# Row biases folded into beta, freer row transposes, longer planned latencies and a new load order in a two-layer graph network

## The chip, the cores and the metric

The kernel runs on one core of one Trainium2 chip. The metric is the device time of one execution in microseconds (us), and every comparison is by the median of several executions. The lines called profile come from one execution recorded by the hardware profiler, whose own time is given beside its span.

## The reference, cut to what matters

There are 64 graphs of 256 nodes with 256 features in fp32, and an adjacency matrix of small integers for each. Two layers follow each other. The first is a graph attention network of two attention steps with a residual, a layer norm, a feed-forward part of 1024 hidden features with ReLU, and a layer norm. The second is a relational attention of 8 heads, and the same feed-forward part with GELU.

```python
# layer 0: two graph attention steps, then a feed-forward part
h = _gat(x, adj, W1, a1, Fout)
h = _gat(h, adj, W2, a2, W2.shape[1])
h = _layernorm(residual + h, g_ln1, b_ln1)
residual2 = h
ff = jnp.matmul(jax.nn.relu(jnp.matmul(h, w_ff1) + b_ff1), w_ff2) + b_ff2
return _layernorm(residual2 + ff, g_ln2, b_ln2)
...
# layer 1: attention over heads with masks by relation, then a feed-forward part
attn_out = out.transpose(0, 2, 1, 3).reshape(Bb, Nn, Dm) @ Wo + bo
x = _ln(src + attn_out, g1, beta1)
ff = jax.nn.gelu(x @ W1 + b1, approximate=False) @ W2 + b2
return _ln(x + ff, g2, beta2)
```

Three biases are added to whole rows just before a residual sum: `b_ff2`, `bo` and `b2`. They are what the change moves.

## The kernel before, in words

The work is cut into 32 pairs of graphs, and everything of a pair stays in SBUF from its loads to its output. All weights are loaded once at the start. The program is straight-line code: it has no loop at run time.

**Stages of a pair.** `whole_way` chains them. `gat_layers` makes the first layer's product (L227), transposes the exponentials `rise` of its scores (L199), weighs (L206, L207) and scales the rows (L212), makes the second layer's first product (L241), repeats the transposes and weights, and ends in the product L253, the residual sum `add_rows` (L266) and `layernorm` (L273 to L282). `feed_forward` first transposes the rows (`rows_transposed`, L289, with ACT's copy to `yT` at L290), makes 8 hidden blocks (L308, with ACT's ReLU or GELU at L311), and four products of the second matrix (L319), again with `add_rows` and `layernorm`. `attention` transposes the rows in the same way, projects queries and keys (L342), values (L335), and goes through four groups of heads: scores (L360), exp on ACT (L365), masking on VectorE (L374), sums (L381), products (L388), and the output product (L405) with a layer norm. A second `feed_forward` and the store of the rows end the pair.

**Where the biases are.** `transposed` has GpSimd (POOL) add the row bias to the residual rows (L292) after the transposes read them, so that the readers of the transposed rows see rows without it.

**The order of the work.** Each pair is a Python generator that yields after every step a tuple (us, later, needs): what the step costs TensorE, how long its result needs until the pair's next step can follow, and the name of a stage that only one pair may be in. `in_turn` keeps three pairs going and issues, step by step, the next of one that is ready by these figures, and takes one outside the feed-forward stage first. The names are "gat", "ff" and "attention"; a pair holds one until `done_with`. So the planner's figures set the order in which instructions of several pairs stand in each engine's queue; the engines then run them in that order, and wait where the figures were too short. In the steady state before, two pairs go through their stages in each 213.4 us.

**Buffers.** `x` and `adjT` have four, `xT` one, `yT` two, `ff` nine, `v` two; `ps` are the eight banks of PSUM.

**The start.** SP's queue first loads pair 0 (`xT`, `adjT`, `x`), then the weights that the setup multiplies (L119), then all layer-norm vectors, then the matrices. `load(pair + 1)` is issued after a pair's first products, so that of pair 1 comes behind the whole list. Each load on the queue also waits for the one that stands eight places ahead of it.

Of the kernel before, what the change touches and what calls it, by code (L numbers as in the profile page):

```python
# [18 lines left out]
P = 128  # L19
# [10 lines left out]
def two_layers(ctx: ExitStack, tc: tile.TileContext, t: dict, out: bass.AP, flag: bass.AP):  # L30
# [32 lines left out]
        nc.sync.dma_start(x, t["x"][rows].rearrange("b (c p) d -> p (b c) d", p=P))  # L63
        return xT, adjT, x

    loaded = {0: load(0)}


    ident = const.tile([P, P], F32, name="ident")
    make_identity(nc, ident)  # L70
# [33 lines left out]
    with tc.tile_pool(name="setup", bufs=1) as setup, \  # L104
# [11 lines left out]
        for m in range(KC):  # L116
# [2 lines left out]
                nc.tensor.matmul(pw[:, :D + 4], lhsT=w1T[:, c, m * P:(m + 1) * P], rhs=right[:, c],  # L119
                                 start=c == 0, stop=c == KC - 1)  # L120
            nc.vector.tensor_copy(w12[:, m], pw[:, :D + 4])
    ln = [tuple(on_all(n, D) for n in names) for names in (
        ("L0_gnn_g_ln1", "L0_gnn_b_ln1"), ("L0_gnn_g_ln2", "L0_gnn_b_ln2"),
        ("L1_gnn_g1", "L1_gnn_beta1"), ("L1_gnn_g2", "L1_gnn_beta2"))]
    ff0 = (weights("L0_gnn_w_ff1"), column("L0_gnn_b_ff1"), weights("L0_gnn_w_ff2"), on_all("L0_gnn_b_ff2", D))
    wq, wk, wo = weights("L1_gnn_Wq"), weights("L1_gnn_Wk"), weights("L1_gnn_Wo")
    wv = const.tile([P, KC, 2, D], F32, name="wv")
    for c in range(KC):
        nc.sync.dma_start(wv[:, c], t["L1_gnn_Wv"][:2, c * P:(c + 1) * P, :].rearrange("r p m -> p r m"))
        nc.vector.tensor_tensor(wv[:, c, 1], wv[:, c, 1], wv[:, c, 0], ALU.subtract)  # L130
    bq, bk = column("L1_gnn_bq"), column("L1_gnn_bk")
    bqs = const.tile([P, KC], F32, name="bqs")
    nc.vector.tensor_scalar(bqs, bq, SCALE, None, ALU.mult)
    bv, bo = on_all("L1_gnn_bv", 2 * D), on_all("L1_gnn_bo", D)
    nc.vector.tensor_tensor(bv[:, D:], bv[:, D:], bv[:, :D], ALU.subtract)
    ff1 = (weights("L1_gnn_W1"), column("L1_gnn_b1"), weights("L1_gnn_W2"), on_all("L1_gnn_b2", D))

    work = ctx.enter_context(tc.tile_pool(name="work", bufs=1))
    small = ctx.enter_context(tc.tile_pool(name="small", bufs=6))
# [1 line left out]

    def bank():
        return psum.tile([P, 512], F32, name="ps")

# [68 lines left out]
    def gat_layers(pair, xT, adjT, x):  # L215
        nc.vector.tensor_reduce(most[:, pair], adjT.bitcast(U32), axis=AX.X, op=ALU.max)
        empty = small.tile([P, 4], F32, name="empty")
        nc.vector.tensor_scalar(empty, most[:, pair], 0.0, EVEN, ALU.is_le, ALU.mult)
        y = work.tile([P, 4, D + 4], F32, name="xw", bufs=2)
        z = work.tile([P, 4, D + 4], F32, name="xw", bufs=2)  # L220
        a, e = [], []
        for b in range(2):
            for j in range(2):
                k = 2 * b + j
                ps = bank()
                for c in range(KC):
                    nc.tensor.matmul(ps[:, :D + 4], lhsT=xT[:, c, k * P:(k + 1) * P], rhs=w12[:, c],  # L227
                                     start=c == 0, stop=c == KC - 1)
                nc.scalar.activation(y[:, k], ps[:, :D + 4], AF.Copy)  # L229
            a.append(addends(y, D + 2, 0, pair, b))  # L230
            yield 1.75, b * 1.6, None
        if pair + 1 < NPAIR:
            loaded[pair + 1] = load(pair + 1)
        for b in range(2):
            e.append(gat_weights(y, D + 2, *a.pop(0), adjT, empty, b))
            yield 0.5, b * 3.4, None
        for b in range(2):
            for i in range(2):
                ps = bank()
                for j in range(2):  # L240
                    nc.tensor.matmul(ps[:, :D + 2], lhsT=e[b][:, j, i * P:(i + 1) * P], rhs=y[:, 2 * b + j, :D + 2],  # L241
                                     start=j == 0, stop=j == 1)
                nc.scalar.activation(z[:, 2 * b + i, :D + 2], ps[:, :D + 2], AF.Copy)
            a.append(addends(z, D, 1, pair, b))
            yield 1.75, 0.4 + b * 0.6, None
        for b in range(2):
            e.append(gat_weights(z, D, *a.pop(0), adjT, empty, b))
            yield 0.5, b * 3.4, None
        for b in range(2):
            ps = bank()  # L250
            for i in range(2):
                for j in range(2):
                    nc.tensor.matmul(ps[:, i * D:(i + 1) * D], lhsT=e[2 + b][:, j, i * P:(i + 1) * P],  # L253
                                     rhs=z[:, 2 * b + j, :D], start=j == 0, stop=j == 1)
            add_rows(x, ps, b)
            layernorm(x, ln[0], b)
            if b == 0:
                yield 1.75, 0.4, None
        done_with("gat")
        yield 1.75, 4.5, "ff"  # L260


    def add_rows(y, p, b):
# [2 lines left out]
        nc.vector.tensor_tensor(rows, p, rows, ALU.add)  # L266

    def layernorm(r, gb, b):
        g, beta = gb
        st, mv = small.tile([P, 2, 6], F32, name="st"), small.tile([P, 2, 2], F32, name="mv")  # L270
        rstd = small.tile([P, 2], F32, name="rstd")
        for j in range(2):
            nc.vector.bn_stats(st[:, j, :], r[:, 2 * b + j, :])  # L273
            nc.vector.bn_aggr(mv[:, j, :], st[:, j, :])
        nc.vector.tensor_scalar(rstd, mv[:, :, 1], EPS, None, ALU.add)  # L275
        nc.gpsimd.tensor_tensor(rstd, rstd, mhalf[:, :2], ALU.pow)  # L276
        for j in range(2):
            row = r[:, 2 * b + j, :]
            nc.vector.scalar_tensor_tensor(row, row, mv[:, j, 0:1], g, op0=ALU.subtract, op1=ALU.mult)
        for j in range(2):  # L280
            row = r[:, 2 * b + j, :]
            nc.vector.scalar_tensor_tensor(row, row, rstd[:, j:j + 1], beta, op0=ALU.mult, op1=ALU.add)  # L282

    def transposed(y, yT, bias, b):

        pt = bank()
        for c in range(KC):
            for j in range(2):
                nc.tensor.transpose(pt[:, c * N + j * P:c * N + (j + 1) * P], y[:, 2 * b + j, c * P:(c + 1) * P], ident)  # L289
        nc.scalar.activation(yT[:, :, b * N:(b + 1) * N], pt.rearrange("p (c n) -> p c n", c=KC), AF.Copy)  # L290
        for j in range(2):
            nc.gpsimd.tensor_tensor(y[:, 2 * b + j, :], y[:, 2 * b + j, :], bias, ALU.add)  # L292

    def rows_transposed(y, bias):
        yT = work.tile([P, KC, 512], F32, name="yT", bufs=2)
        for b in range(2):
            transposed(y, yT, bias, b)
            yield 0.5, 0.5 + b * 0.5, None
        return yT

    def feed_forward(y, w, func, gb):
        w1, b1, w2, b2 = w
        yT = yield from rows_transposed(y, b2)
        f = []
        for m in range(NF):
            p1 = bank()
            for c in range(KC):
                nc.tensor.matmul(p1, lhsT=w1[:, c, m * P:(m + 1) * P], rhs=yT[:, c, :],  # L308
                                 start=c == 0, stop=c == KC - 1)
            h = work.tile([P, 512], F32, name="ff", bufs=NF + 1)  # L310
            nc.scalar.activation(h, p1, func, bias=b1[:, m:m + 1])  # L311
            f.append(h)
            yield 1.72, 0.0, None
        for b in range(2):
            p2 = bank()
            for j in range(2):
                k = 2 * b + j
                for m in range(NF):
                    nc.tensor.matmul(p2[:, j * D:(j + 1) * D], lhsT=f[m][:, k * P:(k + 1) * P], rhs=w2[:, m, :],  # L319
                                     start=m == 0, stop=m == NF - 1)  # L320
                if k < 3:
                    if j == 1:
                        add_rows(y, p2, b)
                        layernorm(y, gb, b)
                    yield 3.44, 0.0, None
        add_rows(y, p2, 1)
        layernorm(y, gb, 1)
        done_with("ff")
# [16 lines left out]
    def attention(y, pair, adjT):  # L345


        yT = yield from rows_transposed(y, bo)
        qT, kT, oT = (work.tile([P, KC, 512], F32, name=n) for n in ("qT", "kT", "oT"))

        def values_tile():
# [72 lines left out]
        for n, (b, c) in enumerate(groups):  # L424
# [7 lines left out]
            if not last:  # L432
                e, ms = ahead, of_relation_1(groups[n + 1][0], ahead)
            divided(b, c, po)
            yield 3.1 if last else 4.1, 3.2 if last else 0.8, None
            if (b, c) == (0, KC - 1):
                v = values_tile()
                for jc in range(2):
                    values(v, jc, N + jc * P, yT)
                    yield 1.72, 0.0, None  # L440
            if n == 2:
                into_rows(0)
                yield 1.75, 0.0, None
        into_rows(1)
        done_with("attention")
        yield 1.75, 4.5, "ff"

    def whole_way(pair):
        yield 0.0, 0.0, "gat"
        xT, adjT, x = loaded.pop(pair)  # L450
        yield from gat_layers(pair, xT, adjT, x)
        yield from feed_forward(x, ff0, AF.Relu, ln[1])
        yield 3.44, 4.5, "attention"
        yield from attention(x, pair, adjT)
        yield from feed_forward(x, ff1, AF.Gelu, ln[3])
        nc.sync.dma_start(out[2 * pair:2 * pair + 2].rearrange("b (c p) d -> p (b c) d", p=P), x)
        yield 3.44, 0.0, None
# [410 lines left out]


_COLUMNS = ("L0_gnn_b_ff1", "L1_gnn_bq", "L1_gnn_bk", "L1_gnn_b1")  # L870


# [24 lines left out]
```

## Time and profile before

| what | us |
|---|---|
| median of 10 executions (3450.32 to 3454.75) | 3453.95 |
| the profiled execution | 3450.91 |
| its span, first to last instruction | 3449.1 |
| TensorE (PE) busy | 3344.3 |
| VectorE (DVE) busy | 1904.3 |
| ScalarE (ACT) busy | 1371.0 |
| GpSimd (POOL) busy | 481.6 |
| DMA queue of the loads and stores, mean share of the 16 engines | 6.9% |

How to read it: busy is the time in which an engine has an instruction running. Matmuls overlap in their pipeline, so their own durations add up to more than the time they take in a row; the distance from one start to the next is the better measure. PEld is the loading of TensorE's weights. A line such as L308 names the source line of the kernel; `out<-in` names the tiles. In a list of waits, an arrow leads from the waiting tile to the one that released it.

### The profile page before, as it was taken

How to read it: one execution, taken by the hardware profiler on the slowest of the kernel's cores; microseconds unless marked ns; L12 is line 12 of the kernel's file. 1: busy time of each engine (PE TensorE's matmuls, PEld its weight loads, DVE VectorE, ACT ScalarE, POOL GpSimd, SP SyncE). 2: the span in 40 equal slices, each digit the busy share in tenths (PEclk: the TensorE clock that was granted, in tenths of full speed). 3: DMA queues.
4: the chain of work that ended last, by engine and by line, in shares of the span. 5: the costliest groups of instructions: out<-in, count | busy, mean ns of one | idle time of the engine just before them, and what ended most of it. 6: DMA issues, size and time to landing. Idle time of an engine off the chain costs nothing.

```text
span 3449.1 us, 47284 instructions
## 1 busy us (share of the span) xinstructions
PE 3344.3 (97%) x18698; PEld 2150.4 (62%) x18698; DVE 1904.3 (55%) x4825; ACT 1371.0 (40%) x2586; POOL 481.6 (14%) x646
## 2 busy tenths in 40 slices
PE   7999999999999999999999999999999999999998
PEld 5566665666656566565665666656666566565655
DVE  5655645556456564555645555465554655546455
ACT  4343343433434334343443434444243442534332
POOL 0201111011110111111111111111111111111110
PEclk9999999999999999999999999999999999999999
DMA  5000010000100001000000100001000010000000
GB/s 166 7 25 19 13 37 7 25 19 13 37 7 25 25 7 37 7 27 24 19 25 7 40 11 25 19 7 43 7 25 19 7 43 7 25 19 1 13 1 14
DMA packets 66868, 78.22 MB, mean 23 GB/s; under 512 B 3280, under 2 KB 57680, under 8 KB 66640
## 3 DMA queue, kind: packets, MB, share of 16 engines
q1 hardware_dynamic: 66640, 75.13, 6.9%
q8 instruction: 150, 2.46, 0.3%
q14 instruction: 78, 0.64, 0.1%
HBM read 58.34 MB, written 16.78 MB: 22 GB/s over the span
## 4 chain that ended last, share of the span: by engine, by line
PE 88%; ACT 9%; DVE 2%; issue 0%; DMA 0%; POOL 0%; SPq 0%; POOLq 0%; DVEq 0%
PE ps L319 26%; PE ps L308 23%; PE ps L342 7%; PE ps L335 6%; PE ps L388 6%; PE ps L360 4%; PE ps L381 4%; PE ps L253 3%; PE ps L405 3%; ACT L189 2%; ACT yT L290 2%; PE ps L241 2%; PE ps L227 2%; PE ps L289 1%; ACT ff L311 1%; DVE e L206 1%
## 5 line engine op out<-in xcount | busy, mean ns | idle before, releaser
L276 POOL TENSOR_TENSOR rstd<-rstd,mhalf 128x2 f32<-128x2 f32 x256 | 206.0, 805 | 2729.5 <-DVE rstd L275 2713.7
L308 PE MATMUL ps<-yT,w_L_gnn_W 128*128 128x512 f32 x1024 | 482.7, 602 | 14.2 <-ACT yT L290 12.5
L308 PE MATMUL ps<-yT,w_L_gnn_w_ff 128*128 128x512 f32 x1024 | 482.5, 602 | 14.1 <-ACT yT L290 12.5
L319 PE MATMUL ps<-w_L_gnn_w_ff,ff 128*128 128x256 f32 x2048 | 450.2, 379 | 0.0
L319 PE MATMUL ps<-w_L_gnn_W,ff 128*128 128x256 f32 x2048 | 449.9, 379 | 0.0
L319 PEld LDWEIGHTS ps<-w_L_gnn_W,ff 128*128 128x128 f32 x2048 | 389.1, 190 | 66.6 <-issue 15.3
L319 PEld LDWEIGHTS ps<-w_L_gnn_w_ff,ff 128*128 128x128 f32 x2048 | 389.0, 190 | 66.0 <-issue 14.8
L374 DVE TENSOR_TENSOR m<-a,adjT 128x512 f32<-128x512 f32 x512 | 327.0, 688 | 175.5 <-ACT a L365 134.8
L266 DVE TENSOR_TENSOR x<-ps,x 128x512 f32<-128x512 f32 x256 | 176.2, 688 | 445.7 <-PE ps L319 330.5
L311 ACT ACTIVATE ff<-ps,c_L_gnn_b_ff 128x512 f32<-128x512 f32 x256 | 176.0, 687 | 448.2 <-PE ps L308 448.2
L365 ACT ACTIVATE a<-ps 128x512 f32<-128x512 f32 x512 | 264.4, 602 | 216.3 <-PE ps L360 216.1
L337 DVE TENSOR_TENSOR v<-ps,b_L_gnn_bv 128x512 f32<-128x512 f32 x128 | 88.1, 689 | 400.4 <-PE ps L335 400.4
L308 PEld LDWEIGHTS ps<-yT,w_L_gnn_W 128*128 128x128 f32 x1024 | 183.0, 190 | 199.2 <-issue 174.1
L308 PEld LDWEIGHTS ps<-yT,w_L_gnn_w_ff 128*128 128x128 f32 x1024 | 183.1, 190 | 198.9 <-issue 174.1
L290 ACT ACTIVATE yT<-ps 128x512 f32<-128x512 f32 x192 | 110.3, 593 | 479.6 <-PE ps L289 479.6
L311 ACT ACTIVATE ff<-ps,c_L_gnn_b 128x512 f32<-128x512 f32 x256 | 175.9, 687 | 292.8 <-PE ps L308 292.4
L335 PE MATMUL ps<-wv,yT 128*128 128x512 f32 x512 | 235.4, 592 | 0.0
L229 ACT ACTIVATE xw<-ps 128x260 f32<-128x260 f32 x128 | 45.7, 379 | 456.5 <-PE ps L227 456.5
L394 DVE RECIPROCAL s<-ps 128x256 f32<-128x256 f32 x128 | 224.1, 1751 | 0.0
L273 DVE BATCH_NORM_STATS2 st<-x 128x6 f32<-128x256 f32 x512 | 192.8, 419 | 8.7
L206 DVE SCALAR_TENSOR_TENSOR e<-ps,ratio,up 128x256 f32<-128x256 f32 x256 | 115.7, 475 | 141.5 <-ACT up L201 141.5
L335 PEld LDWEIGHTS ps<-wv,yT 128*128 128x128 f32 x512 | 97.3, 190 | 122.5 <-issue 122.2
(81 smaller groups left out, 4290.3 us busy)
## 6 DMA issues: line engine op xcount, KB each, us to landing
xT<-in_xT SPq DMA_DIRECT2D x32, 512.0 KB, 4.6
adjT<-in_adjT SPq DMA_DIRECT2D x32, 512.0 KB, 3.9
x<-in_x SPq DMA_DIRECT2D x32, 512.0 KB, 4.1
out<-x SPq DMA_DIRECT2D x32, 512.0 KB, 3.2
w_L_gnn_w_ff<-in_L_gnn_w_ff SPq DMA_DIRECT2D x2, 1024.0 KB, 9.3
w_L_gnn_W<-in_L_gnn_W SPq DMA_DIRECT2D x2, 1024.0 KB, 8.4
wv<-in_L_gnn_Wv SPq DMA_DIRECT2D x2, 256.0 KB, 7.2
w_L_gnn_W1T<-in_L_gnn_W1T SPq DMA_DIRECT2D x1, 256.0 KB, 6.8
```

Of the source, the lines that this page charges most:

```text
L273: nc.vector.bn_stats(st[:, j, :], r[:, 2 * b + j, :])
L276: nc.gpsimd.tensor_tensor(rstd, rstd, mhalf[:, :2], ALU.pow)
L290: nc.scalar.activation(yT[:, :, b * N:(b + 1) * N], pt.rearrange("p (c n) -> p c n", c=KC), AF.Copy)
L308: nc.tensor.matmul(p1, lhsT=w1[:, c, m * P:(m + 1) * P], rhs=yT[:, c, :], start=c == 0, stop=c == KC - 1)
L311: nc.scalar.activation(h, p1, func, bias=b1[:, m:m + 1])
L319: nc.tensor.matmul(p2[:, j * D:(j + 1) * D], lhsT=f[m][:, k * P:(k + 1) * P], rhs=w2[:, m, :], start=m == 0, stop=m == NF - 1)
L335: nc.tensor.matmul(ps, lhsT=yT[:, c, at:at + P], rhs=wv[:, c].rearrange("p r m -> p (r m)"), start=c == 0, stop=c == KC - 1)
L342: nc.tensor.matmul(ps, lhsT=w[:, d, c * P:(c + 1) * P], rhs=yT[:, d, :], start=d == 0, stop=d == KC - 1)
L365: nc.scalar.activation(a, ps[o], AF.Exp)
L374: nc.vector.tensor_tensor(m, a, adj, ALU.mult)
L388: nc.tensor.matmul(po[o * DH:(o + 1) * DH, :N], lhsT=v[:, jc, at:at + DH], rhs=ms[o][:, jc * N:(jc + 1) * N], start=r == 0 and jc == 0, st ...
L394: nc.vector.reciprocal(s, po[:, N:])
```

## The change

It has five parts. The row bias is added once, at the start, to the beta of the layer norm that makes the rows, and the GpSimd additions go. The readers of those rows then see the bias as well, so their own biases are lowered by the bias times their weights: `relieve` and `relieve_attention` make these products once, for pair 0, ahead of the stage that reads them. The row transposes are issued before the stage "ff" or "attention" is free, and the stage is asked for only after the second of them; `yT` has a third buffer. Several `later` figures of the planner are larger, and the second graph's values come one head group earlier. Last, pair 0's loads come after the setup's weights, the other loads stand in the order of their stages, and there are three more small ones (the same biases as columns).

```diff
+    loaded = {0: load(0)}
+    def layernorm_weights(g, beta, more=None):
+        return on_all(g, D), on_all(beta, D), more and (on_all(more, D), column(more + "c"))
+    ln = [layernorm_weights("L0_gnn_g_ln1", "L0_gnn_b_ln1", "L0_gnn_b_ff2")]
+    ff0 = (weights("L0_gnn_w_ff1"), column("L0_gnn_b_ff1"), weights("L0_gnn_w_ff2"))
+    ln.append(layernorm_weights("L0_gnn_g_ln2", "L0_gnn_b_ln2", "L1_gnn_bo"))
+    wq, wk = weights("L1_gnn_Wq"), weights("L1_gnn_Wk")
...
+    bq, bk, bv = column("L1_gnn_bq"), column("L1_gnn_bk"), on_all("L1_gnn_bv", 2 * D)
...
+    wo = weights("L1_gnn_Wo")
+    ln.append(layernorm_weights("L1_gnn_g1", "L1_gnn_beta1", "L1_gnn_b2"))
+    ff1 = (weights("L1_gnn_W1"), column("L1_gnn_b1"), weights("L1_gnn_W2"))
+    ln.append(layernorm_weights("L1_gnn_g2", "L1_gnn_beta2"))
+    for gbm in ln[:3]:
+        nc.vector.tensor_tensor(gbm[1], gbm[1], gbm[2][0], ALU.add)
...
+    def relieve(bias, w, more):
+        p = bank()
+        of = w.shape[-1] // P
+        for m in range(of):
+            for c in range(KC):
+                nc.tensor.matmul(p[:, m:m + 1], lhsT=w[:, c, m * P:(m + 1) * P], rhs=more[1][:, c:c + 1],
+                                 start=c == 0, stop=c == KC - 1)
+        nc.vector.tensor_tensor(bias, bias, p[:, :of], ALU.subtract)
+    def relieve_attention(more):
+        relieve(bq, wq, more)
+        relieve(bk, wk, more)
+        nc.vector.tensor_scalar(bqs, bq, SCALE, None, ALU.mult)
+        p = bank()
+        for c in range(KC):
+            nc.tensor.matmul(p, lhsT=more[1][:, c:c + 1].to_broadcast([P, P]),
+                             rhs=wv[:, c].rearrange("p r m -> p (r m)"), start=c == 0, stop=c == KC - 1)
+        nc.vector.tensor_tensor(bv, bv, p, ALU.subtract)
...
             e.append(gat_weights(y, D + 2, *a.pop(0), adjT, empty, b))
-            yield 0.5, b * 3.4, None
+            yield 0.5, b * 4.4, None
...
             e.append(gat_weights(z, D, *a.pop(0), adjT, empty, b))
-            yield 0.5, b * 3.4, None
+            yield 0.5, b * 4.4, None
...
         done_with("gat")
-        yield 1.75, 4.5, "ff"
+        yield 1.75, 6.0, None
...
-        for j in range(2):
-            nc.gpsimd.tensor_tensor(y[:, 2 * b + j, :], y[:, 2 * b + j, :], bias, ALU.add)
...
+    def rows_transposed(y, needs):
+        yT = work.tile([P, KC, 512], F32, name="yT", bufs=3)
...
+            yield 0.5, 0.5 + b * 0.8, needs if b else None
...
-            yield 3.1 if last else 4.1, 3.2 if last else 0.8, None
-            if (b, c) == (0, KC - 1):
-                v = values_tile()
+            yield 3.1 if last else 4.1, 4.8 if last else 0.8, None
+            if n == 0:
+                following = values_tile()
                 for jc in range(2):
-                    values(v, jc, N + jc * P, yT)
+                    values(following, jc, N + jc * P, yT)
                     yield 1.72, 0.0, None
+            if n == 1:
+                v = following
...
         done_with("attention")
-        yield 1.75, 4.5, "ff"
+        yield 1.75, 6.0, None
...
         yield from gat_layers(pair, xT, adjT, x)
+        if pair == 0:
+            relieve(ff0[1], ff0[0], ln[0][2])
         yield from feed_forward(x, ff0, AF.Relu, ln[1])
-        yield 3.44, 4.5, "attention"
+        yield 3.44, 6.0, None
+        if pair == 0:
+            relieve_attention(ln[1][2])
         yield from attention(x, pair, adjT)
+        if pair == 0:
+            relieve(ff1[1], ff1[0], ln[2][2])
         yield from feed_forward(x, ff1, AF.Gelu, ln[3])
```

More of the change, by code (lines that the diff above doesn't have):

```diff
@@ L64, in load @@
         return xT, adjT, x
-    loaded = {0: load(0)}
     ident = const.tile([P, P], F32, name="ident")
@@ L121, in two_layers @@
             nc.vector.tensor_copy(w12[:, m], pw[:, :D + 4])
[L122 to L126, printed above, removed]
+    loaded = {0: load(0)}
[5 more added lines that the diff above has]
+    wq, wk = weights("L1_gnn_Wq"), weights("L1_gnn_Wk")
     wv = const.tile([P, KC, 2, D], F32, name="wv")
@@ L130, in two_layers @@
         nc.vector.tensor_tensor(wv[:, c, 1], wv[:, c, 1], wv[:, c, 0], ALU.subtract)
-    bq, bk = column("L1_gnn_bq"), column("L1_gnn_bk")
+    bq, bk, bv = column("L1_gnn_bq"), column("L1_gnn_bk"), on_all("L1_gnn_bv", 2 * D)
     bqs = const.tile([P, KC], F32, name="bqs")
-    nc.vector.tensor_scalar(bqs, bq, SCALE, None, ALU.mult)
-    bv, bo = on_all("L1_gnn_bv", 2 * D), on_all("L1_gnn_bo", D)
     nc.vector.tensor_tensor(bv[:, D:], bv[:, D:], bv[:, :D], ALU.subtract)
-    ff1 = (weights("L1_gnn_W1"), column("L1_gnn_b1"), weights("L1_gnn_W2"), on_all("L1_gnn_b2", D))
+    wo = weights("L1_gnn_Wo")
[4 more added lines that the diff above has]
+        nc.vector.tensor_tensor(gbm[1], gbm[1], gbm[2][0], ALU.add)
     work = ctx.enter_context(tc.tile_pool(name="work", bufs=1))
@@ L268, in layernorm @@
     def layernorm(r, gb, b):
-        g, beta = gb
+        g, beta, _ = gb
         st, mv = small.tile([P, 2, 6], F32, name="st"), small.tile([P, 2, 2], F32, name="mv")
@@ L282, in layernorm @@
             nc.vector.scalar_tensor_tensor(row, row, rstd[:, j:j + 1], beta, op0=ALU.mult, op1=ALU.add)
-    def transposed(y, yT, bias, b):
-        pt = bank()
-        for c in range(KC):
-            for j in range(2):
-                nc.tensor.transpose(pt[:, c * N + j * P:c * N + (j + 1) * P], y[:, 2 * b + j, c * P:(c + 1) * P], ident)
-        nc.scalar.activation(yT[:, :, b * N:(b + 1) * N], pt.rearrange("p (c n) -> p c n", c=KC), AF.Copy)
-        for j in range(2):
-            nc.gpsimd.tensor_tensor(y[:, 2 * b + j, :], y[:, 2 * b + j, :], bias, ALU.add)
-    def rows_transposed(y, bias):
-        yT = work.tile([P, KC, 512], F32, name="yT", bufs=2)
-        for b in range(2):
-            transposed(y, yT, bias, b)
-            yield 0.5, 0.5 + b * 0.5, None
+    def rows_transposed(y, needs):
+        yT = work.tile([P, KC, 512], F32, name="yT", bufs=3)
+        for b in range(2):
+            pt = bank()
+            for c in range(KC):
+                for j in range(2):
+                    nc.tensor.transpose(pt[:, c * N + j * P:c * N + (j + 1) * P],
+                                        y[:, 2 * b + j, c * P:(c + 1) * P], ident)
+            nc.scalar.activation(yT[:, :, b * N:(b + 1) * N], pt.rearrange("p (c n) -> p c n", c=KC), AF.Copy)
+            yield 0.5, 0.5 + b * 0.8, needs if b else None
         return yT
     def feed_forward(y, w, func, gb):
-        w1, b1, w2, b2 = w
-        yT = yield from rows_transposed(y, b2)
+        w1, b1, w2 = w
+        yT = yield from rows_transposed(y, "ff")
         f = []
@@ L345, in attention @@
     def attention(y, pair, adjT):
-        yT = yield from rows_transposed(y, bo)
+        yT = yield from rows_transposed(y, "attention")
         qT, kT, oT = (work.tile([P, KC, 512], F32, name=n) for n in ("qT", "kT", "oT"))
@@ L870 @@
 _COLUMNS = ("L0_gnn_b_ff1", "L1_gnn_bq", "L1_gnn_bk", "L1_gnn_b1")
+_ROWS_AND_COLUMNS = ("L0_gnn_b_ff2", "L1_gnn_bo", "L1_gnn_b2")
 def kernel(**inputs):
@@ L884 @@
     laid["adjT"] = np.ascontiguousarray(adj.transpose(0, 2, 1))
+    for k in _ROWS_AND_COLUMNS:
+        laid[k + "c"] = np.ascontiguousarray(laid[k].reshape(-1, P).T)
     for k in _COLUMNS:
```

## The prediction

> **What bounds the kernel now.** First the page's head and busy table, then the waits of TensorE, then stretches of its timeline.
>
> ```profile
> span 3449.1 us, 47284 instructions
> PE 3344.3 (97%) x18698; PEld 2150.4 (62%) x18698; DVE 1904.3 (55%) x4825; ACT 1371.0 (40%) x2586; POOL 481.6 (14%) x646
> PE 88%; ACT 9%; DVE 2%; issue 0%; DMA 0%; POOL 0%; SPq 0%; POOLq 0%; DVEq 0%
> ```
>
> TensorE (PE) is busy 97% of the span, and the chain that ended last is 88% PE and 9% ACT. A change gains by shortening PE's stream or by closing its gaps. The waits of PE after the first 50 us (engine, line and tile waiting, releaser: total us, times, longest):
>
> ```profile
> PE ps L199 <- ACT rise L189: 29.0, 44, 0.9
> PE ps L308 <- ACT yT L290: 24.3, 33, 0.7
> PE ps L253 <- ACT xw L212: 18.0, 15, 1.2
> PE ps L289 <- DVE x L282: 0.7, 2, 0.5
> PE ps L405 <- DVE oT L398: 0.2, 1, 0.2
> ```
>
> That is 72.2 us, nearly all waiting for ACT, in three places that recur once or twice in every pair of graphs. The PE timeline of one steady stretch shows them (start us, us, what, and the idle before it):
>
> ```profile
> 1718.97 1.04 PE L289 MATMUL ps<-ident,x 128*128 128x128 f32 x8
> 1719.84 0.60 PE L199 MATMUL ps<-ident,rise 128*128 128x128 f32 x4
> 1720.97 0.65 PE L199 MATMUL ps<-ident,rise 128*128 128x128 f32 x4 [0.52 <-ACT rise L189]
> 1721.73 3.70 PE L308 MATMUL ps<-yT,w_L_gnn_W 128*128 128x512 f32 x8
> ...
> 1732.18 0.60 PE L199 MATMUL ps<-ident,rise 128*128 128x128 f32 x4
> 1733.70 0.65 PE L199 MATMUL ps<-ident,rise 128*128 128x128 f32 x4 [0.92 <-ACT rise L189]
> 1734.19 3.60 PE L308 MATMUL ps<-yT,w_L_gnn_W 128*128 128x512 f32 x8
> 1738.98 1.99 PE L253 MATMUL ps<-xw,e 128*128 128x256 f32 x8 [1.20 <-ACT xw L212]
> ...
> 1776.51 1.04 PE L199 MATMUL ps<-ident,rise 128*128 128x128 f32 x8
> 1777.38 3.60 PE L308 MATMUL ps<-yT,w_L_gnn_w_ff 128*128 128x512 f32 x8
> ...
> 1801.52 1.04 PE L289 MATMUL ps<-ident,x 128*128 128x128 f32 x8
> 1803.29 3.70 PE L308 MATMUL ps<-yT,w_L_gnn_w_ff 128*128 128x512 f32 x8 [0.74 <-ACT yT L290]
> 1806.83 0.60 PE L289 MATMUL ps<-ident,x 128*128 128x128 f32 x4
> ```
>
> A wait costs more than its idle time, since the pipeline also drains: I measure from start to start. Eight uncovered transposes of `rise` take 1777.38 - 1776.51 = 0.87. The first stop (after the first layer's product) takes 1.89, so costs 1.02, plus 0.10 in the FF products after it (groups of 3.70 beside 3.60). The second (after the second layer's product, GELU beside it) takes 2.01: 1.14. The third takes 4.79 where eight FF products take 3.44: 1.35, plus 0.11 in its own group. The row transposes take 1.77 to the first projection where eight take 0.87: 0.90, plus 0.10.
>
> **What the Trainium skill says.** "ScalarE: Activation LUTs", section What ACT_TABLE_LOAD costs, puts a switch of function set at 1283 ns for the load and 1380 ns for a drain. The trace agrees on the load (1283 ns mean), not on the drain: at 1727.61 a load starts and the next activation starts 1.30 later. "TensorE: Matmul & The Clock Gate", section LDWEIGHTS, says that a weight load takes columns / 1.2 ns, so 107 ns for 128 columns; here a load lasts 141 to 190 ns, but consecutive transposes start 0.87 / 8 = 0.109 us apart, which fits. "SBUF — State Buffer", section Who interferes with whom, says that VectorE and GpSimd exclude each other on a shared port pair; the trace agrees: while POOL adds a bias at 42.27, two steps of L282 take 1.88 instead of 0.88.
>
> **The change part by part.**
>
> *Covering the waits.* The order of the built program was compared step by step with the one of before. Before, 33 layer-norm row pairs after the start are transposed and at once read by the first projection (33 x 1.00 = 33.0). 29 times the first layer's products are followed only by short transposes (29 x 1.12 = 32.5). 15 graph pairs have GELU beside their second layer (15 x (1.14 + 1.46) = 39.0). Sum 104.5. After it:
> - Row transposes stand among other pairs' steps, with at least 1.72 before the projection, in all but three places: pair 0 (before has that one in its start), and pairs 30 and 31 at the end. Left: 2 x 1.00.
> - An FF step (1.72) now stands between the first layer's product and its transposes. Before, the waiting transposes start 1720.97 - 1718.97 = 2.00 after the product ends; after, 1.72 + 0.43 = 2.15 lie before them. I take 0; at worst 0.3 each.
> - Between the second layer's weights and the last products stand two FF steps and 3.44 of the next part, 6.9 instead of the 4.8 that were needed: 0.
> - The transposes after the second layer's product keep their cover of one FF step. The cause there is ACT, in order: exp table, GELU table, exp table between two graphs. This stop stays, and the new rhythm (three pairs in three stages) puts GELU beside 20 graph pairs instead of 15: 20 x 1.14 = 22.8.
>
> In its place the row reciprocals, the up copies and three GELUs stand ahead of the scaling L212 in ACT's queue before the first layer's second product; counted in the rows' durations the scaling is ready 0.4 before PE arrives. I take 0, up to 0.3 x 20.
>
> *GpSimd.* 384 bias additions go (93.2 + 92.5 + 90.5 = 276 us of POOL). They hide behind PE wholly; POOL is 0% of the chain. VectorE's slowed layer norms delay PE by 0.7 in all, so the gain is between 0 and 0.7; I take 0. No one waits for the value any more, and nothing is late next.
>
> *Bias corrections for pair 0.* 16 + 8 + 16 products of two instructions each with one moving column, 80 in all, and four of 512 columns. No row shows a one-column product with a full weight load. From below 0.109 (transposes), from above 0.190 (the load's length laid end to end): 8.7 to 15.2; I take 8.7. The four wide ones take 4 x 0.43 = 1.7. All lie on PE: 10.4. The VectorE subtractions behind them are small, and the readers (first GELU or Relu, first queries) have at least 0.9 of transposes and their evacuation before them: 0. Three additions to beta (0.42 each on VectorE) lie in the start, where VectorE has gaps; two of them queue for late bias loads, ahead of pair 0's second layer and its layer norm, and are covered by the load of the second pair below.
>
> *Loads in the order of need.* Before, the first product waits 12.02 for its weights, and pair 1's first product at 38.08 waited for its xT. Now four loads come first. The first product can start some 4 us earlier, but the stages of pair 0 then run to the same gate: the xT of pair 1 is still the last load of the list on SP, behind 35 loads instead of 32, each waiting for the one eight places ahead. Loads 8 to 33 took 24.2 us to issue, 0.97 each, so three more cost up to 2.9; the bytes hardly grow and the small ones are spread. I take 1.5 later, between -3 (the transfers close ranks) and +5. So the 4 us are lost in a longer wait for that transfer.
>
> *The rest.* A third yT buffer, the values of the second graph one group earlier and the raised latencies only enter the order. PE's other steps and switches between tile shapes keep their number: 0. At the end, pair 30's rows are transposed 3.87 after the attention output, whose layer norm needs about 4.2 (4.0 from addition to last step in the trace, and the hand-over): 0.3.
>
> *Sum.* The profiled execution took 3450.9, span 3449.1 and 1.8 around it. 3450.9 - 104.5 + 22.8 + 2.0 + 0.3 + 10.4 + 1.5 = 3383.4. The median of before is 3.0 above its profiled execution; so 3386.
>
> **The rivals.**
> - *The waits move.* In attention PE meets ACT's exps, VectorE's masking and eight PSUM banks; two groups now follow each other where the values stood between. For: under GELU, ACT needs 1.28 + 0.69 + 1.28 + 2.4 = 5.65 a group and PE 5.5. Against: the same spacing stood between the first groups before, without a listed wait. With 0.3 to 1.5 in each of 32 attentions: 3396 to 3434.
> - *The clock takes it back.* A denser PE may be granted less: at 0.98 instead of 0.999, 3383 grows by 2%, and the time is about 3453, no change. Against: PEclk is 9 in all 40 slices at 97% busy.
> - *ACT's table switches become the bound* (slower). Every stage with GELU has six switches of 1.28. If the queue behind them fell so far back that each of 20 stages stopped PE for 6 us instead of 1.14: 3386 + 20 x 4.9 = 3483. It decides from (104.5 - 14.2) / 20 = 4.5 each. Against: ACT's work in such a stage, some 24 us, is well under the stage's 43.
> - *Better.* ACT, no longer delayed by earlier queues, also covers the remaining 22.8: 3363.
>
> **How the numbers follow.** Forecast 0.72, moved waits 0.14, clock 0.04, slower 0.04, better 0.06. 0.2% is about what a measurement of this kernel can tell from no change. Faster: 0.72 + 0.14 + 0.06 = 0.92; same 0.04; slower 0.04. The forecast's own bounds: -4.5 (start) gives 3381, and the better case pulls the low end to 3372; upwards 6.5 (products) + 3.5 (start) + 9 + 6 (uncertain covers) give 3411, and the milder half of the moved waits 3420. Left out: clock, slower, and the ends of two cases, together under 0.2.
>
> **What would show it.** L308 waiting for yT falls from 33 times to 3; L253's wait for L212 is gone; the L199 waits are about 20, of 0.9 each; POOL has 384 instructions fewer; the new products take about 10 us; pair 1's first product starts within some 3 us of 38 and waits longer for its DMA. The forecast is wrong if waits appear at the attention's products (L381, L388), at the first layer's second product or on PSUM banks, if the L199 waits grow beyond 1.2, or if the clock row drops.

## The result, and the profile after

The changed kernel takes 3384.95 us (median of 8, 3383.59 to 3385.91) against 3454.3 us of the kernel before (median of 28, 3449.67 to 3454.97): a ratio of 0.9801, 95% interval 0.9792 to 0.9810. The profiled execution took 3384.1, its span is 3382.2. The lines of its page that answer to those of before:

```profile
span 3382.2 us, 46922 instructions
PE 3333.7 (99%) x18782; PEld 2160.3 (64%) x18782; DVE 1863.1 (55%) x4833; ACT 1367.3 (40%) x2576; POOL 203.1 (6%) x262
PE 95%; ACT 4%; DMA 1%; SPq 0%; issue 0%; DVE 0%; POOL 0%; POOLq 0%; DVEq 0%
```

PE has 84 instructions more and is busy 99% instead of 97%; ACT's share of the chain fell from 9% to 4%, DVE's from 2% to 0%. POOL has 384 instructions fewer. The lines of the code have moved: the transposes of `rise` are now L225 (L199), the first projection L330 (L308), the first layer's second product L267 (L241), the last products L279 (L253), the output product L427 (L405). PE's waits after the first 55 us are two rows:

```profile
PE ps L225 <- ACT rise L215: 18.4, 20, 0.9
PE ps L330 <- ACT yT L319: 1.4, 2, 0.7
```

Those are the counts forecast: 20 and 2. A steady stretch of PE's timeline, with GELU beside a graph layer, shows where the others went:

```profile
1861.65 1.88 PE L330 MATMUL ps<-yT,w_L_gnn_W 128*128 128x512 f32 x4
1863.37 1.04 PE L225 MATMUL ps<-ident,rise 128*128 128x128 f32 x8
...
1874.59 1.88 PE L330 MATMUL ps<-yT,w_L_gnn_W 128*128 128x512 f32 x4
1876.31 0.60 PE L225 MATMUL ps<-ident,rise 128*128 128x128 f32 x4
1877.83 0.65 PE L225 MATMUL ps<-ident,rise 128*128 128x128 f32 x4 [0.92 <-ACT rise L215]
1878.31 3.60 PE L330 MATMUL ps<-yT,w_L_gnn_W 128*128 128x512 f32 x8
...
1885.20 1.89 PE L279 MATMUL ps<-xw,e 128*128 128x256 f32 x8
```

A projection step (L330) stands ahead of the first transposes, whose eight run in one group without a stop. The second set still stops at its second half, 0.92 of idle time as before. The last products L279 come 1885.20 - 1878.31 = 6.89 after those transposes and wait for nothing.

The start of the changed kernel:

```profile
8.08 3.83 PE L117 MATMUL pw<-right,w_L_gnn_W1T 128*128 128x260 f32 x8 [8.08 <-DVE junk L111]
37.85 3.77 PE L253 MATMUL ps<-w,xT 128*128 128x260 f32 x16 [3.65 <-DMA xT<-in_xT]
...
42.92 3.82 PE L157 MATMUL ps<-c_L_gnn_b_ff2c,w_L_gnn_w_ff 128*128 128x1 f32 x32
46.60 1.95 PE L317 MATMUL ps<-ident,x 128*128 128x128 f32 x8
49.24 3.78 PE L330 MATMUL ps<-yT,w_L_gnn_w_ff 128*128 128x512 f32 x4 [0.69 <-ACT yT L319]
```

The first product comes 3.94 earlier than before (12.02), pair 1's first product only 0.23 earlier (38.08), after a wait of 3.65 instead of 0.76. The 32 one-column products last from 42.92 to 46.60. Behind them four projections take 3.78 instead of the 1.88 to 1.98 of the steady state: the granted clock is low, 0.62 and 0.70 in the two rows below (stretch; length; busy time and instructions of PE, PEld, DVE, ACT, POOL; granted clock; DMA share; GB/s), where before has 1.00.

```profile
45.00:50.00 5.00, 4.31 (x23) 3.65 (x24) 3.51 (x13) 1.99 (x4) 0.00 (x0) 0.62 0.32 108
50.00:55.00 5.00, 5.00 (x13) 2.84 (x12) 0.00 (x0) 1.89 (x5) 0.00 (x0) 0.70 0.00 0
```

### The profile page after: what moved, and what is told of

The parts are those of the page before. It is cut to its first block, busy times and chain, and to the rows that moved or that the text cites. A ratio compares the mean times of both kernels' runs of the same rounds, so it can differ in the third digit from the quotient of the medians.

```text
span 3382.2 us, 46922 instructions
## 1 busy us (share of the span) xinstructions
PE 3333.7 (99%) x18782; PEld 2160.3 (64%) x18782; DVE 1863.1 (55%) x4833; ACT 1367.3 (40%) x2576; POOL 203.1 (6%) x262
## 4 chain that ended last, share of the span: by engine, by line
PE 95%; ACT 4%; DMA 1%; SPq 0%; issue 0%; DVE 0%; POOL 0%; POOLq 0%; DVEq 0%
PE ps L341 26%; PE ps L330 25%; PE ps L364 7%; PE ps L410 7%; PE ps L357 6%; PE ps L382 4%; PE ps L403 4%; PE ps L427 3%; PE ps L253 3%; PE ps L279 3%; PE ps L317 3%; PE ps L267 2%; ACT L215 2%; PE ps L225 1%; ACT L333 1%; ACT xw L269 1%
## 5 line engine op out<-in xcount | busy, mean ns | idle before, releaser
L330 PE MATMUL ps<-yT,w_L_gnn_w_ff 128*128 128x512 f32 x1024 | 480.0, 601 | 0.7 <-ACT yT L319 0.7
L330 PE MATMUL ps<-yT,w_L_gnn_W 128*128 128x512 f32 x1024 | 472.4, 596 | 1.4 <-ACT yT L319 1.4
L341 PE MATMUL ps<-w_L_gnn_w_ff,ff 128*128 128x256 f32 x2048 | 458.0, 381 | 0.0
L341 PE MATMUL ps<-w_L_gnn_W,ff 128*128 128x256 f32 x2048 | 456.8, 380 | 0.0
L330 PEld LDWEIGHTS ps<-yT,w_L_gnn_W 128*128 128x128 f32 x1024 | 185.3, 190 | 179.0 <-issue 173.7
L330 PEld LDWEIGHTS ps<-yT,w_L_gnn_w_ff 128*128 128x128 f32 x1024 | 182.1, 190 | 178.9 <-issue 175.9
L211 DVE TENSOR_REDUCE steep<-xw 128x1 f32<-128x4 f32 x128 | 19.8, 155 | 255.1 <-ACT xw L269 210.6
```

## The experiments

Theory: the gain is closed gaps, each closed because the planner puts enough other work between a producer and its reader; the biases only cost, and the loads are neutral. Rivals: the freed transposes do it alone; or the bias move does, by taking GpSimd off the rows; or the new load order contributes.

Each was run five times (e2 21 times, e6 13 times) beside the kernel before, whose median was 3454.0 to 3454.6 us. Differences of whole runs are of medians; places inside a run are read from its one profiled execution.

**e1: only the longer latencies** (with the stage names still asked for ahead of the transposes)

```diff
-            yield 0.5, b * 3.4, None
+            yield 0.5, b * 4.4, None
-        yield 1.75, 4.5, "ff"
+        yield 1.75, 6.0, "ff"
-            yield 3.1 if last else 4.1, 3.2 if last else 0.8, None
+            yield 3.1 if last else 4.1, 4.8 if last else 0.8, None
...
```

> The kernel before with only the planner's longer latencies. Theory (the gain comes from TensorE's three waits on ACT that the order of steps covers): this gives one more feed-forward step ahead of the last products of the graph layers, and covers that wait alone: 15 x 1.46 = 21.9 us less, 3432. The other two waits stay: 33 of yT, 44 of rise. Rival 1 (the gain is that of the removed GpSimd work): no change, 3454. Rival 2 (the gain is all in the latencies): about 3385.

Measured: 3438.68 us, ratio 0.9956 (0.9942 to 0.9970), so -15.3. The 15 waits before the last products became one of 4.5; the waits for `rise` (28.8) and yT (25.1) stayed.

**e2: only the freed row transposes and the third yT**

```diff
-            yield 0.5, 0.5 + b * 0.5, None
+            yield 0.5, 0.5 + b * 0.5, needs if b else None
-        yield 1.75, 4.5, "ff"
+        yield 1.75, 4.5, None
...
```

> The kernel before with only the freed row transposes (the stage is asked for after the second of them) and the third yT buffer. Theory: the waits for yT go (33.0), and since three pairs now mix, a feed-forward step stands before the first layer's transposes (32.5 go); GELU stands beside 19 graph pairs instead of 15, so the second-layer wait and the one before the last products grow to 19 x 1.14 and 19 x 1.46 (4.6 and 5.8 more). Sum 55.1 less: 3399. Rival 1: 3454. Rival 2: 3454.

Measured: 3448.65 us, ratio 0.9985 (0.9978 to 0.9991), so -5.4 where some 55 were expected. Its waits after the first 55 us, with the line numbers of before:

```profile
PE ps L253 <- ACT xw L212: 22.8, 19, 1.2
PE ps L241 <- ACT xw L212: 22.4, 19, 1.2
PE ps L199 <- ACT rise L189: 17.5, 19, 0.9
PE ps L405 <- DVE oT L398: 16.3, 28, 0.7
```

The 33 waits for yT are gone as meant, but rows L241 and L405 are new (L405 had 0.2), and L253 grew from 15 to 19 places. With the new rhythm the old latencies are too short: 3.4 is satisfied by two feed-forward steps (3.44), and 3.2 by one part of the second matrix (3.44).

**e3: the planner's part whole** (e1 and e2 together, and the values one head group earlier; biases and loads as before)

> The kernel before with all of the planner's part (latencies, freed row transposes, earlier values), but with the biases still added to rows by GpSimd and the loads in the old order. Theory: all of the covers, without the 10.8 us that the bias products take in the changed kernel: 3454.3 - 104.5 + 22.8 + 2.3 = 3375, faster than the changed kernel. Rival 1 (the biases and GpSimd are what gains): near 3454, or between.

Measured: 3375.01 us, ratio 0.9773 (0.9760 to 0.9787), so -79.0. The parts alone give -15.3 and -5.4; together, with the values' earlier place, they give nearly four times that. It is also 9.9 less than the changed kernel, which has the bias move and the new load order on top.

**e9 and e10: which latency serves which wait.** Both are e2 plus a part of the latencies: e9 the `b * 4.4`, e10 all the others.

> The run with the freed row transposes alone (3448.65 us), and of the longer latencies only that of the two transposes of rise (b * 4.4 in place of b * 3.4). My theory of why that run gained 5 us and not 55: the freed transposes bring two waits that told latencies must cover. 4.4 puts a third feed-forward step before graph 0's products, so the waits at L241 and L253 for the softmax's scale (27.4 and 27.9 us of lost PE time in that run's trace, 19 places each) go and the ones at L405 (24.2 us) stay: 3448.65 - 51 to 55 = 3394 to 3398 us. Rival: the waits only move one product later, with the third step: 3440 us or more.

> The run with the freed row transposes alone (3448.65 us), and of the longer latencies all but that of the transposes of rise: 6.0 after a stage, 4.8 before the attention's last output product, 0.8 between the row transposes. My theory: 4.8 puts two feed-forward parts before the last output product, so the 28 waits at L405 (24.2 us of lost PE time) go, and the ones at L241 and L253 (55 us) stay: 3424 us. Rival: freed transposes that come late by the longer 6.0 bring back the waits for yT: 3440 us or more.

Measured: e9 3400.58 us, ratio 0.9846 (0.9832 to 0.9859); e10 3431.0 us, ratio 0.9934 (0.9921 to 0.9948). The waits of e9, then of e10, after the first 55 us:

```profile
PE ps L405 <- DVE oT L398: 17.5, 28, 1.3
PE ps L199 <- ACT rise L189: 17.4, 19, 0.9
PE ps L388 <- DVE v L337: 3.2, 2, 2.3
```

```profile
PE ps L253 <- ACT xw L212: 23.9, 20, 1.2
PE ps L241 <- ACT xw L212: 23.5, 20, 1.2
PE ps L199 <- ACT rise L189: 18.4, 20, 0.9
...
```

The 4.4 removes the rows L241 and L253; the other latencies, the 4.8 before the last output product among them, remove L405. e9 is 2.6 above its range (two new waits for the values, 3.2). e10 is 7 above its figure. By the count below, L405 had cost 20.9 and not the 24.2 expected; GELU meets 20 graph pairs and not 19, so that the rows left over grew by 3.6; and two waits for yT came back, 1.7.

No run moves the values alone, and none adds the third yT alone. Against before, e9 and e10 gain 48.6 and 18.2 more than e2, 66.8 together, and e3 gains 73.6 more. So some 7 us are left for the earlier values, whose 3.2 of waits in e9 are gone in e3, and for what the parts do to each other; the record doesn't share them out.

What PE lost is counted below, by place: the distance from each matmul's start to the next, less the distance that the same pair of shapes keeps undisturbed, where over 0.15 us, after 55 us. The attention's inner groups are left out, where the switches of shape, near 308 us, are the same in all (3.6 more in e9, the waits for values, stand under other).

| us lost at | before | e1 | e2 | e9 | e10 | e3 | after |
|---|---|---|---|---|---|---|---|
| transposes of `rise` | 36.2 | 36.0 | 20.6 | 20.5 | 21.6 | 21.6 | 21.7 |
| first layer's second product | 0 | 0 | 25.4 | 0 | 26.8 | 0 | 0 |
| last products | 20.4 | 6.3 | 25.9 | 0 | 27.1 | 0 | 0 |
| first projection (yT) | 37.8 | 38.7 | 0 | 0.8 | 1.7 | 1.7 | 1.7 |
| output product (oT) | 0 | 0 | 20.9 | 22.1 | 0 | 0 | 0 |
| other | 1.0 | 0 | 0 | 4.0 | 0.5 | 0.5 | 1.1 |
| sum | 95.4 | 81.0 | 92.8 | 47.4 | 77.7 | 23.8 | 24.5 |
| sum against before | | -14.4 | -2.6 | -48.0 | -17.7 | -71.6 | -70.9 |
| measured against before | | -15.3 | -5.4 | -54.0 | -23.6 | -79.0 | -69.4 |

The count explains the order and most of the size. What it misses are mostly losses of about 0.1 per group that lie under its bound: with the bound at 0.10 the same count gives 15.8, 3.6, 52.3, 21.5 and 79.6 less for e1, e2, e9, e10 and e3, within 2.1 of what was measured. The 1.1 under other in the changed kernel lies in its half-clock window at 166 to 169 us. The changed kernel has e3's gaps and pays for its products.

**e4: only the biases moved**

> The kernel before with only the biases moved (beta, the products for pair 0, no GpSimd additions), its order of loads and its planner kept but for three more small loads. Theory: the products add 10.8 us to TensorE's stream, the removed GpSimd work gives back at most 0.7: 3464. Rival 1: clearly below 3454.

Measured: 3469.51 us, ratio 1.0049 (1.0035 to 1.0063), so +15.5. The waits of the steady state are unchanged. The profiled executions of the two differ by more, 18.6, since that of before was 3 us under its median. Of this, 3.3 comes ahead of pair 1's first product (41.42 instead of 38.08): the three more loads stand ahead of its xT, which is issued at 32.18 instead of 28.76. 15.3 comes behind it: 11.4 for the products, some of them at half clock, and the rest with low clock, five windows of 3.41 us there where before has none. Over the whole run e4 has seven such windows after the first rise of the clock, and before has one. Taking GpSimd's additions away gains little: the 0.7 of waits for x in before is gone.

**e8: the changed kernel without the one-column products**

```diff
-            relieve(ff0[1], ff0[0], ln[0][2])
-            relieve_attention(ln[1][2])
+            nc.vector.tensor_scalar(bqs, bq, SCALE, None, ALU.mult)
-            relieve(ff1[1], ff1[0], ln[2][2])
```

> The changed kernel without the one-column products and their subtractions; it leaves out the correction of the readers' biases. By the products' own time in the trace (3.68 + 0.81 + 0.89 + 1.80 + 3.59 = 10.8 us) the time is 3374 us. My theory: the half-clock stretches right after the products (46 to 53 us and 166 to 169 us) are caused by them, and go too, some 4 us more: 3370 us. Rival: those stretches come from the start alone: 3374 us, and the stretches stay where they were.

Measured: 3371.36 us (3370.72 to 3371.43), ratio 0.9763 (0.9750 to 0.9776): 13.6 below the changed kernel, so 2.8 more than the products' own time in its trace, 10.8. The half-clock stretches at 46 to 53 and 166 to 169 us are gone; one of two windows has appeared at 19.6 to 26.4 us, in the start. From pair 1's first product (38.95, in the changed kernel 37.85) to the end e8 is shorter by 14.5: the 10.8, and 3.7 with three half-clock windows fewer. The start, 1.1 later, hides a part of this.

**e7: the first 32 products moved into the wait for pair 1's xT**

```diff
+        if pair == 0:
+            relieve(ff0[1], ff0[0], ln[0][2])
         done_with("gat")
```

> The changed kernel with the 32 one-column products of L0_gnn_w_ff1 issued at the end of pair 0's graph layer, ahead of pair 1's first products, where TensorE waits 3.65 us for xT of pair 1, in place of before pair 0's first feed-forward layer. My theory: 3.6 us of products lie inside that wait, so 3381 us, and less by another 1 to 3 us if the half-clock stretch that follows these products falls into the wait too. Rival: the start is paced by the loads behind them, so the time is only given back at the next product that needs a weight: 3385 us.

Measured: 3382.05 us (3381.15 to 3384.25), ratio 0.9796 (0.9783 to 0.9810): 2.9 below the changed kernel, whose lowest run is 3383.59, so the ranges still overlap. The products start at 36.63, ahead of pair 1's at 40.12, which then wait for nothing, and the clock stays at 1.00 behind them.

**e6: only the loads reordered**

> The kernel before with only the loads reordered (inputs of pair 0 after the weights that the first product needs, the other weights in the order of need), nothing else. My theory: TensorE's first product comes about 4 us earlier, and all of it is given back in the wait for xT of pair 1, which the trace of the changed kernel shows as 3.65 us in place of 0.76: 3454 us, within 1 of the kernel before. Rival: the start is gained for the most part, 3450 us, because the wait for xT of pair 1 is the price of another part of the change.

Measured: 3451.24 us, ratio 0.9993 (0.9985 to 1.0001). That lies between my theory and the rival, and the interval reaches no change. In its trace the first product starts at 7.74 and pair 1's at 37.63, so 4.28 are gained and all but 0.45 given back there: 2.6 in the first products of pair 0, which came before the clock's first rise at 17.4 (6.36 instead of 3.77), 1.1 in a longer wait of the last products for ACT, and 0.2 in the wait for xT.

**e5: two feed-forward steps ahead of the second transposes**, on the changed kernel

```diff
-            yield 1.75, 0.4 + b * 0.6, None
+            yield 1.75, 0.4 + b * 1.8, None
```

> The changed kernel with the second-layer products' latency of graph 1 told as 0.4 + b * 1.8 in place of 0.4 + b * 0.6, so that under a GELU stage two feed-forward steps (about 5.6 us with what lies between) stand between graph 1's second-layer products and its transposes of rise in place of one. My theory: the 20 waits of 0.9 us before these transposes (21.7 us in all) go and nothing else becomes late: 3362 us, and the waits of L225 after the start are near 0. Rival: the distance is taken from the last products of the graph layer (L279), which then wait for e or for the softmax's scale: 3380 to 3390 us, with 20 waits at L279.

Measured: 3365.21 us (3364.31 to 3368.06), ratio 0.9749 (0.9736 to 0.9762): 19.7 below the changed kernel. Its waits after the first 55 us, and the stretch that answers to the one shown of the changed kernel:

```profile
PE ps L330 <- ACT yT L319: 2.0, 3, 0.7
PE ps L427 <- DVE oT L420: 1.4, 1, 1.4
```

```profile
1866.65 3.60 PE L330 MATMUL ps<-yT,w_L_gnn_W 128*128 128x512 f32 x8
1870.09 1.04 PE L225 MATMUL ps<-ident,rise 128*128 128x128 f32 x8
1870.96 1.88 PE L330 MATMUL ps<-yT,w_L_gnn_W 128*128 128x512 f32 x4
```

Eight projections stand ahead of the transposes instead of four, and these run in one group. The 20 waits are gone, and the last products did not become late. The lost time by the count above falls from 24.5 to 4.1.

**e11 and e12: the best of these put together.** e11 is e3 with the edit of e5. e12 adds the new load order, and loads pair 1's xT right behind the first feed-forward weights, for which xT has two buffers.

```diff
+        xT = io.tile([P, KC, 512], F32, name="xT", bufs=2)
...
+    early = {1: load_xT(1)}
+    ln.append((on_all("L0_gnn_g_ln2", D), on_all("L0_gnn_b_ln2", D)))
```

> The planner's part alone (3375.01 us) with 0.4 + b * 1.8 in place of 0.4 + b * 0.6: the bias products and the order of the loads stay as in the kernel before. If the two edits add up: 3375.0 - 19.8 (what the second edit gave on the changed kernel) = 3355 us.

> The kernel of e11 with the loads in the order of need, and with xT in two buffers, so that pair 1's xT is loaded ahead of the attention's weights and not after all of them. My theory: the start's gain of 4 us (8.1 in place of 12.0 us to the first product) is now kept, because the wait for xT of pair 1 goes: 3351 us, pair 1's first product at about 34.5 us, with no wait for its DMA. Rival: the time of the start is set by the bytes that have to land before the first feed-forward layer, so the wait reappears at the next load: 3355 us.

Measured: e11 3355.15 us (3353.18 to 3357.47), ratio 0.9713 (0.9699 to 0.9726); e12 3352.22 us (3351.70 to 3353.97), ratio 0.9706 (0.9693 to 0.9719). e11 is where two adding gains put it. The start of e12:

```profile
7.42 3.70 PE L120 MATMUL pw<-right,w_L_gnn_W1T 128*128 128x260 f32 x8 [7.42 <-DVE junk L114]
...
32.92 3.67 PE L234 MATMUL ps<-w,xT 128*128 128x260 f32 x16
...
41.00 3.26 PE L315 MATMUL ps<-yT,w_L_gnn_w_ff 128*128 128x512 f32 x4 [0.69 <-ACT yT L297]
```

Pair 1 starts at 32.92 with no wait for its transfer. Some is given back behind it: pair 0's transposes wait 0.95 for the layer norm, and the first projections at 41.00 run at half clock. The gain of 2.9 over e11 is near the spread of the runs. e12 beats both kernels: it is 1.0% below the changed one, and it does so without the bias move.

## Why the prediction was right, point by point

**The covers: right in place and size.** The sum had 104.5 less for all waits closed, 22.8 for the second transposes' stop that stays, 2.0 for two waits at the end and 0.3 for the tail: 79.4 less. The planner's part alone measured 79.0 less (e3). The waits that stay are 20 of 0.9 and 2 of 0.7 as forecast, and neither place that I took at nothing with an upper bound (first transposes, first layer's second product) waits. The cause given for the stop that stays is ACT's order with its table switches. The trace of before has it ahead of the transposes that wait until 1733.70:

```profile
1729.50 1.28 ACT L311 ACT_TABLE_LOAD   x1
1730.80 0.69 ACT L311 ACTIVATE ff<-ps,c_L_gnn_b 128x512 f32<-128x512 f32 x1
1731.38 0.65 ACT L243 ACTIVATE xw<-ps 128x258 f32<-128x258 f32 x2
1732.06 1.28 ACT L189 ACT_TABLE_LOAD   x1
1733.35 0.30 ACT L189 ACTIVATE rise<-xw,shift 128x2 f32<-128x2 f32 x1
```

ACT goes without a pause through two table loads, a GELU and two copies before it makes `rise`. Beside ReLU, at 1773 to 1776, there is no load, ACT waits for PE, and the eight transposes at 1776.51 run in one group. No run took the loads away, so this is read from the trace and not tried. e5 shows that a second step of 1.72 covers the stop, for a gain of 19.7 where the term of the sum was 22.8. The difference is mostly two new places: 1.6 at the output product and 0.8 more at the first projection.

**The parts don't add, which the sum did not tell.** It gave each closed wait its own size as if it could be had alone. For the whole change that holds, for its parts it doesn't: my expectation of e2, made from the same terms, was 3399, and 3448.65 was measured. Freeing the transposes changes which stage of one pair runs beside which of another, and then short latencies cost at places that were covered before. The prediction was right because it counted the order of the whole program.

**The bias products: right by themselves, a term was missing.** 10.4 was forecast: 80 at 0.109 and four at 0.43. The trace has 3.68 + 3.59 + 0.81 + 0.89 + 1.80 = 10.8, so 0.101 to 0.115 for each of the 80; the lower bound, not the load's length of 0.190, was the right choice. (Loads of L199 last 136 ns, so the range given for a load should begin there and not at 141.) What was missing is the clock, which the forecast left at full speed behind the products: e8 is 13.6 faster, not 10.8, and 14.5 from pair 1's first product on.

The Trainium skill, "TensorE: Matmul & The Clock Gate", section What's actually happening, says that the clock is full or half by how busy the array was in a window of 3413 ns that runs freely. The traces agree: every stretch of half clock here, from the first rise to PE's last work, is a multiple of 3.413 us. The four kernels with the products (changed, e4, e5, e7) have 4, 7, 4 and 3 such windows after the first rise, the other ten (before among them) 1 to 3. In each of these four, two groups of 32 products can be laid on that grid of windows, continued from the recorded edges. Where the products fill 0.72 or more of one window (both groups of the changed kernel and of e4, the first of e5, the second of e7), the next window is at half clock; where they are cut by an edge so that no window is filled above 0.57 (the second of e5, the first of e7), it stays full. So how much the products cost beyond their own time seems to depend on where the window happens to lie. e8 shows that the low stretches behind the products go with them; the rule of the filled window was found afterwards in these eight groups, and no run tests it. Why the clock falls behind products that occupy PE without a gap is not settled: that a column product leaves the array little to do is argued, not shown.

**The start: its size was off.** I took +1.5, between -3 and +5. The gate was as described, the xT of pair 1, with a wait that grew to 3.65. Where it lies differs from trace to trace. Pair 1's first product came at 38.08 to 39.50 in the seven traces with the old order and 32 loads, at 37.63 in e6 (new order, 32 loads), at 37.85, 38.95 and 38.55 in the changed kernel, e8 and e5 (new order, 35 loads), and at 41.42 in e4 (old order, 35 loads). So three loads more cost 1.9 to 3.3 in the old order, near the 2.9 taken at most; in the new one the 0.2 to 1.3 between e6 and these three lie within the spread of traces of one order, 1.4. e8 less e3, the new load order and the missing GpSimd work together, is -3.6; e6 alone is -3.1 with an interval that reaches 0. So the loads likely gained up to 3 us, at the low end of my range, and how much isn't settled: in the two profiled executions before and e6 differ by 0.4 in span.

**GpSimd: right.** 0 to 0.7 was forecast for 276 us of POOL taken away, and no run shows a gain beyond that; none takes it away alone.

**The sum, in what was measured:** 3454.3 - 79.0 (e3) - 3.6 (e8 less e3) + 13.6 (changed kernel less e8) = 3385.3, against 3384.95. These three steps lead from before to the changed kernel, so their sum has to come out: it shares the gain out and proves nothing. A sum of separate runs is e3, e4 and e6: 3454.3 - 79.0 + 15.5 - 3.1 = 3387.7, 2.8 too high. By the shares, the forecast 3386 was close to within 1 partly by luck: products and clock were 3.2 too low, loads 5.1 too high, and the two errors mostly cancelled.

**The rivals.** Moved waits did not appear at the attention's products in the whole change; the mechanism was real, though, and e2 and e9 show it at the output product and, twice in e9, at the values. The clock did not fall in the steady state at 99% busy (0.997 for the span), only in the first 170 us. The table switches stayed at 0.92 of idle time per stage, far from the 4.5 where they would decide. The better case did not come by itself, but e5 came near it (3365.21 against 3363) by one more changed figure.

## What to carry to other kernels

When a planner decides the order, count the work that stands between each producer and its reader in the whole new order: a dependency taken away changes what runs beside what, and latencies that were long enough become too short. A wait that remains at the same place in every round is then worth one more step of told latency, as long as what follows has cover to give. Work moved into the start can cost more than its own time, as the clock behind the column products shows. e7 puts a part of it into a wait that is there anyway, and took 2.9 less.

## What the runs showed of the hardware that was not expected

- The clock's first rise came 10.9 to 20.9 us after the span's start in the 14 traces, 2.9 to 9.6 us after the first product, and a product group of the first graph layer took 6.36 (e6) or 3.77 (before) by it. A difference of this size, 2.6, limits what can be told of the start.
- A product with one moving column and a full load of weights takes 0.101 to 0.115 us, about as long as a transpose of 128 columns (0.109): the moving columns are not what it pays for.
